# Layer 0's exponentials: from four shared PSUM banks to five SBUF tiles of their own

## The chip, the core and the metric

The kernel runs on one core of one Trainium2 chip. The metric is the device time of one execution in microseconds, from launch to the end of the last instruction; lower is better. Times before are of three runs and of one more execution that the hardware profiler recorded. Engines: PE is TensorE (PEld its weight loads), DVE is VectorE, ACT is ScalarE, POOL is GpSimd, SP is SyncE, which here only issues DMAs.

## The reference

Four layers run one after the other over an image tensor `x` of 4 x 64 x 64 x 128 in float32, each as `x = x + layer(groupnorm(x))`. Only layer 0 is touched. It is a selective scan over the image in four directions:

```python
def step(h, xs):
    ut, dt, bt, ct = xs
    dA = jnp.exp(dt[..., None] * A)
    h = dA * h + (dt * ut)[..., None] * bt[:, :, None, :]
    y = jnp.einsum('bkdn,bkn->bkd', h, ct)
    return (h, y)
```

There are 256 channels `d`, 16 states `n` for each, four directions `k` (rows, columns, and both backwards) and 4096 positions, for each of four images. In front of the scan stand a projection, a 3x3 convolution for each channel and a SiLU; `delta` is a softplus. Behind it the four directions are summed, normalized over the channels, gated and projected. Layers 1 to 3 (Fourier layers and attention) follow.

## The kernel before

**Tiling.** Layer 0 (`layer0`) works in units: image `b`, direction `k` (in the order 1, 3, 0, 2), chunk `c` of `CH` = 512 positions: 4 x 4 x 8 = 128 units. Channels lie on the 128 partitions in two halves `s`. Inside a unit a loop runs over the 16 states `n`; each pass of it is called a step here, 2048 in all. A step does:

- POOL: `dB = du * Bb` for both halves at once (line 413), 128x1024. `du` is `delta * u`, made once for each unit (line 299). `Bb` is a row of B broadcast to all partitions by a DMA, four states at a time (three buffers); `dB` has three buffers.
- ACT: for each half `dA = exp(delta * A)` (line 420), 128x512.
- DVE: for each half one scan instruction (line 421), `h[t] = dA[t] * h[t-1] + dB[t]`, from `dA` and `dB`, starting from `state`, a column in SBUF. `h` lies in SBUF, three buffers of four states.
- PE and ACT, seven steps later (`LAG`): `transpose` turns `h` (line 318, PE, into PSUM; line 322, ACT, copies `hT` to SBUF), and `products` multiplies with `W`, which holds C (line 363), into `yT`.

At four steps of a unit PE makes `cr` (line 433), and DVE makes `W` from it (line 436). The next unit's inputs are prepared in between: `xd_ps` (line 277, PE), its copy `xd` (line 279, ACT), `dp` (line 286, PE), `delta` (lines 292 and 293 on ACT, 296 on DVE), `du` (POOL). After each group of four states POOL copies the last column of `h` into `state` (lines 446 and 451). `before(b + 1)` (normalization, projection, convolution of the next image) and `after(b)` (line 236, a normalization on DVE; line 250, `yg`, a product on POOL; the output projection) are generators, of which the loop takes a piece at most steps.

**Buffers.** PSUM has eight banks. Pool `ps` holds two for the transposes, `psy` two for `yT`. Pool `psx` holds four under the one tag `x`: `dA` takes two tiles a step out of it, and `cr`, `xd_ps`, `dp` and the small matmuls of `before` and `after` take theirs from the same four in turn. A new tile of a tag waits until the readers of the tile four places before it are done. SBUF tiles come from `tmp`.

```python
        tmp = pool("l0tmp", 2)
        ...
        ps = pool("l0ps", 2, space=PSUM)
        psx = pool("l0psx", 4, space=PSUM)
        psy = pool("l0psy", 1, space=PSUM)
```

**Order.** The loop is inside `tc.manual_schedule(engines=order)` for PE, ACT, DVE and POOL: each of these runs its instructions in the order of the code, and an instruction that waits holds up everything behind it on its engine. DMAs are issued by SP's queue, whose order a scheduler sets.

Of the kernel before, what the change touches and what calls it, by code (L numbers as in the profile page):

```python
# [10 lines left out]
F32 = mybir.dt.float32  # L11
# [5 lines left out]
P = 128  # L17
# [5 lines left out]
CH = 512  # L23
# [58 lines left out]
def layer0(sh, A, x_in, x_out, scr):  # L82
# [6 lines left out]
    with ExitStack() as ctx:  # L89
        pool = lambda name, bufs, **kw: ctx.enter_context(tc.tile_pool(name=name, bufs=bufs, **kw))  # L90
        wp = pool("l0w", 1)
        tmp = pool("l0tmp", 2)
        small = pool("l0small", 2)
        ps = pool("l0ps", 2, space=PSUM)
        psx = pool("l0psx", 4, space=PSUM)
# [168 lines left out]
        def fetch(b, k, c):  # L264

            u = tmp.tile([P, 2, CH], F32, name="u")
            pc = NCH - 1 - c if k >= 2 else c
            nc.sync.dma_start(
                u, scr(f"xw{b % 2}" if k % 2 else f"xr{b % 2}")[:, :, pc * CH : (pc + 1) * CH].rearrange("s p t -> p s t")
            )  # L270
            return u, (u[:, :, ::-1] if k >= 2 else u)

        def inputs(k, c, u):

            xd_ps = psx.tile([40, CH], F32, name="xd_ps", tag="x")
            for s in range(2):
                nc.tensor.matmul(xd_ps, lhsT=w_x[:, s, k, :], rhs=u[:, s, :], start=(s == 0), stop=(s == 1))  # L277
            xd = xds[c % 2]
            nc.scalar.copy(xd[0:40, :], xd_ps)  # L279
            bd = scr(f"B{(NCH * k + c) % 3}")  # L280
            nc.sync.dma_start(bd, xd[8:24, :])
            yield
            dps = []
            for s in range(2):
                dp = psx.tile([P, CH], F32, name="dp", tag="x")
                nc.tensor.matmul(dp, lhsT=w_dt[:, k, s * P : (s + 1) * P], rhs=xd, start=True, stop=True)  # L286
                dps.append(dp)
                yield
            delta = tmp.tile([P, 2, CH], F32, name="delta")

            for s in range(2):
                nc.scalar.activation(delta[:, s, :], dps[s], AF.Exp)
            nc.scalar.activation(delta, delta, AF.Ln, bias=1.0)
            yield
            for s in range(2):
                nc.vector.scalar_tensor_tensor(delta[:, s, :], delta[:, s, :], 88.0, dps[s], ALU.min, ALU.max)  # L296
            yield
            du = tmp.tile([P, 2, CH], F32, name="du")
            nc.gpsimd.tensor_tensor(du, delta, u, ALU.mult)  # L299
            yield xd, bd, delta, du  # L300
# [24 lines left out]
        def transposed(G):  # L325

            nonlocal copied
            todo, copied = copied, None
            if G is not None:
                q = G["q"]  # L330
                G["q"] += 1
                hTs = [transpose(G, q, 0)]
                copied = G, q, hTs
            yield
            if todo is not None:
                products(*todo)
            if G is not None:
                hTs.append(transpose(G, q, 1))
            yield
# [49 lines left out]
        with tc.manual_schedule(engines=order):  # L389
            for i, (b, k, c) in enumerate(units):  # L390
# [14 lines left out]
                for n in range(NS):  # L405
                    g, q = divmod(n, 4)
                    if q == 0:
                        Bb = tmp.tile([P, 4, CH], F32, name="Bb", bufs=3)
                        nc.sync.dma_start(Bb, bd[4 * g : 4 * g + 4, :].partition_broadcast(P))
                        h = tmp.tile([P, 2, CH, 4], F32, name="h", bufs=3)  # L410
                        G = dict(unit=unit, g=g, h=h, q=0)
                    dB = tmp.tile([P, 2, CH], F32, name="dB", bufs=3)
                    nc.gpsimd.tensor_tensor(dB, du, Bb[:, q : q + 1, :].to_broadcast([P, 2, CH]), ALU.mult)  # L413
                    behind = iter(())
                    if NS * i + n >= LAG:
                        H = queue[0]
                        behind = transposed(H)
                    for s in range(2):
                        dA = psx.tile([P, CH], F32, name="dA", tag="x")
                        nc.scalar.activation(dA, delta[:, s, :], AF.Exp, scale=A_neg[:, k, s, n : n + 1])  # L420
                        nc.vector.tensor_tensor_scan(  # L421
                            h[:, s, :, q], dA, dB[:, s, :], state[:, s, n : n + 1], ALU.mult, ALU.add
                        )
                        next(behind, None)
                    if n == 1:
                        for f in ends.pop("state", []):
                            f()
                    if queue and queue[0]["q"] == 4:
                        queue.pop(0)
                    if n in (1, 5, 11, 13):  # L430
                        crg = (1, 5, 11, 13).index(n)
                        cr = psx.tile([P, CH], F32, name="cr", tag="x")
                        nc.tensor.matmul(cr, lhsT=sel[:, crg, :], rhs=xd[0:40, :], start=True, stop=True)  # L433
                    if n in (2, 6, 12, 14):
                        W = tmp.tile([P, 16, 32], F32, name="W", bufs=3)
                        nc.vector.tensor_tensor(  # L436
                            W,
                            cr.rearrange("p (a t) -> p a t", t=32),
                            diag[:, int(rev) : int(rev) + 1, :].to_broadcast([P, 16, 32]),
                            ALU.mult,  # L440
                        )
                        Ws[crg] = W
                    if q == 3:
                        queue.append(G)
                    if c < NCH - 1 and q == 2 and g > 0:
                        nc.gpsimd.tensor_copy(state[:, :, 4 * g - 4 : 4 * g], last[:, :, CH - 1, :])
                    if q == 3:
                        last = h
                        if g == 3 and c < NCH - 1:
                            ends["state"] = [  # L450
                                lambda st=state, l=h: nc.gpsimd.tensor_copy(st[:, :, 12:16], l[:, :, CH - 1, :])
                            ]

                    if i + 1 < len(units):
                        if n == 3:
                            u_next, v_next = fetch(*units[i + 1])
                        if n in (7, 8, 9):
                            coming = coming or inputs(*units[i + 1][1:], v_next)
                            next(coming)
                        if n in (10, 11):  # L460
                            next(coming)
                        if n == 15:
                            ready = next(coming)

                    if n == 10:
                        y = unit["y"] = tmp.tile([P, 4, 2 * P], F32, name="y", tag="t4", bufs=4)
                        if k == 0:
                            src = scr("y3").rearrange("(w q r) d -> r w q d", w=64, r=2)
                            for r in range(2):
                                nc.sync.dma_start(y[64 * r : 64 * r + 64], src[r, :, 4 * c : 4 * c + 4, :])  # L470
                        elif k != 1:
                            nc.sync.dma_start(y, dst(1 if k == 3 else 0))

                    if n not in (1, 5, 8, 9, 11, 13) and pieces:
                        if next(pieces[0], None) is None:
                            pieces.pop(0)
# [1239 lines left out]
```

## Time and profile before

| | us |
|---|---|
| median of three runs | 9474.88 (9465.93 to 9475.91) |
| profiled execution, its own time | 9466.91 |
| its span, first to last instruction | 9465.1 |
| stretch of layer 0's scans, 218.6 to 6968.7 | 6750 |
| mean granted TensorE clock | 0.889 |

Busy time of the engines, over the span and in the stretch of the scans:

| engine | span, us | stretch of the scans, us |
|---|---|---|
| PE | 7878.8 (83%) | 5817.4 |
| DVE | 7035.5 (74%) | 5736.7 |
| ACT | 6403.3 (68%) | 5370.6 |
| POOL | 5610.1 (59%) | 5237.7 |

A line of the costliest groups gives source line, engine, operation, output and inputs with their tile names, shapes, how often it ran, then after the bar busy time in us and the mean duration of one in ns, then the idle time of the engine just in front of these instructions and what ended most of it. A line of a timeline gives start and duration in us, engine, line and operation; in brackets stands idle time in front. In a tile's answer, three durations are minimum, median and maximum in ns. An instruction's duration in this profile includes time in which it has been started and is held up inside its engine, so a longer duration is not always more work. Layer 2's helper records each of its operations under line 785, so its groups are told apart by tile names.

### The profile page before, as it was taken

The numbers are of one execution on the slowest core, as the hardware profiler recorded it, in microseconds if no ns is written. First come the engines' busy times: TensorE is split into PE (matmuls) and PEld (weight loads), VectorE is DVE, ScalarE is ACT, GpSimd is POOL, SyncE is SP. The second block draws the span as 40 slices with busy tenths as digits, with TensorE's granted clock in tenths as the row PEclk, the third lists the DMA queues.
The fourth block names the chain that finished last, engine by engine and source line by source line (L and its number), as shares of the span: only waits on it lengthen the run. The fifth ranks groups of instructions, "written<-read, shape, count | busy, mean of one in ns | idle before, by whom it ended". The sixth has DMA issues, their size and how long they took to land. (4 is left out here: it accounts for less than half of the span.)

```text
span 9465.1 us, 144952 instructions
## 1 busy us (share of the span) xinstructions
PE 7878.8 (83%) x54256; PEld 4499.6 (48%) x54256; DVE 7035.5 (74%) x8298; ACT 6403.3 (68%) x11773; POOL 5610.1 (59%) x2998
## 2 busy tenths in 40 slices
PE   7888888888888888888888888888869967677588
PEld 3444444444444444444444444444447756365366
DVE  1778788898887788888777898998954553443578
ACT  2878787777787777778777777888842211614467
POOL 1777778877777777777777878888840001010133
PEclk8989998888898998889999898999979988778699
DMA  6334443333444443334434333333332124131333
GB/s 112 110 115 127 115 128 123 113 121 128 125 126 118 117 122 115 136 121 119 118 118 126 110 137 123 130 128 114 131 116 53 35 59 132 51 103 50 88 87 86
DMA packets 1148677, 1038.13 MB, mean 110 GB/s; under 512 B 564127, under 2 KB 1001979, under 8 KB 1081156
## 3 DMA queue, kind: packets, MB, share of 16 engines
q1 hardware_dynamic: 1146292, 1027.13, 35.7%
q8 instruction: 426, 6.98, 0.3%
q14 instruction: 279, 2.29, 0.1%
q10 hardware_dynamic: 1680, 1.74, 0.1%
HBM read 845.18 MB, written 181.32 MB: 108 GB/s over the span
## 5 line engine op out<-in xcount | busy, mean ns | idle before, releaser
L421 DVE TENSOR_TENSOR_SCAN h<-dA,state,dB 128x512 f32<-128x512 f32 x4096 | 4998.3, 1271 | 1003.1 <-ACT dA L420 786.5
L413 POOL TENSOR_TENSOR dB<-du,Bb 128x1024 f32<-128x1024 f32 x2048 | 4829.1, 2374 | 1413.6 <-DVE h L421 1146.7
L420 ACT ACTIVATE dA<-delta,A_neg 128x512 f32<-128x512 f32 x4096 | 2864.3, 699 | 505.2 <-DVE h L421 428.5
L318 PEld LDWEIGHTS pt<-ident,h 128*128 128x128 f32 x16384 | 1948.6, 150 | 2008.3 <-issue 1303.5
L318 PE MATMUL pt<-ident,h 128*128 128x128 f32 x16384 | 2756.7, 299 | 103.8 <-ACT hT L322 103.8
L322 ACT COPY hT<-pt 128x512 f32<-128x512 f32 x4096 | 2416.9, 590 | 588.5 <-PE pt L318 552.9
L363 PE MATMUL yT<-hT,W 128*32 128x256 f32 x16384 | 1660.3, 418 | 18.0 <-ACT hT L322 15.2
L433 PE MATMUL cr<-xd,sel 40*128 40x512 f32 x1024 | 667.6, 736 | 460.5 <-DVE h L421 456.3
L363 PEld LDWEIGHTS yT<-hT,W 128*32 128x32 f32 x16384 | 409.7, 111 | 576.2 <-issue 374.0
L193 PE MATMUL cv<-pad,taps 128*128 128x512 f32 x1152 | 608.2, 629 | 0.0
L433 PEld LDWEIGHTS cr<-xd,sel 40*128 40x128 f32 x1024 | 169.4, 207 | 565.8 <-DVE h L421 514.4
L785 POOL TENSOR_TENSOR xg<-xg,so 128x1024 f32<-128x1024 f32 x8 | 26.6, 3343 | 693.4 <-ACT so L785 672.3
L1434 POOL TENSOR_TENSOR S<-S,sm 128x784 f32<-128x784 f32 x128 | 191.1, 1493 | 408.7 <-DVE sm L1432 348.4
L277 PE MATMUL xd_ps<-u,w_x 128*40 128x512 f32 x512 | 281.5, 678 | 134.2 <-DVE h L421 106.1
L286 PE MATMUL dp<-xd,w_dt 65*128 65x512 f32 x512 | 282.2, 634 | 113.6 <-DVE h L421 112.8
L299 POOL TENSOR_TENSOR du<-delta,u 128x1024 f32<-128x1024 f32 x128 | 304.0, 2375 | 66.3 <-DVE delta L296 66.3
L436 DVE TENSOR_TENSOR W<-cr,diag 128x512 f32<-128x512 f32 x512 | 341.4, 667 | 0.0
L785 POOL TENSOR_TENSOR z<-z,sp 128x1024 f32<-128x1024 f32 x16 | 41.8, 2616 | 465.4 <-ACT z L785 465.1
L1441 ACT ACTIVATE S<-S,mx 128x196 f32<-128x196 f32 x512 | 227.9, 448 | 33.9 <-DVE mx L1468 33.4
L785 PE MATMUL pz<-PT,WX 128*68 128x64 f32 x2048 | 167.1, 248 | 100.0 <-DVE WX L785 81.4
L193 PEld LDWEIGHTS cv<-pad,taps 128*128 128x128 f32 x1152 | 197.1, 203 | 106.1 <-issue 99.4
L279 ACT COPY xd<-xd_ps 40x512 f32<-40x512 f32 x128 | 74.3, 580 | 223.2 <-PE xd_ps L277 223.2
(333 smaller groups left out, 7785.7 us busy)
## 6 DMA issues: line engine op xcount, KB each, us to landing
Bb<-l_B SPq DMA_DIRECT2D x512, 1024.0 KB
l_y<-y SPq DMA_DIRECT2D x128, 512.0 KB
wr<-wt SPq DMA_DIRECT2D x256, 136.0 KB
u<-l_xw SPq DMA_DIRECT2D x64, 512.0 KB
y<-l_y SPq DMA_DIRECT2D x64, 512.0 KB
u<-l_xr SPq DMA_DIRECT2D x64, 512.0 KB
V<-l_v SPq DMA_DIRECT2D x512, 49.0 KB
l_xr<-xo SPq DMA_DIRECT2D x64, 256.0 KB
```

The lines of the kernel that those rows point to most:

```text
L193: nc.tensor.matmul(pm, lhsT=taps[:, s, t, :], rhs=pad[:, s, dy : dy + 8, dx : dx + 64], start=(t == 0), stop=(t == 8),)
L277: nc.tensor.matmul(xd_ps, lhsT=w_x[:, s, k, :], rhs=u[:, s, :], start=(s == 0), stop=(s == 1))
L286: nc.tensor.matmul(dp, lhsT=w_dt[:, k, s * P : (s + 1) * P], rhs=xd, start=True, stop=True)
L299: nc.gpsimd.tensor_tensor(du, delta, u, ALU.mult)
L318: nc.tensor.transpose(pt[:, r, s, :], G["h"][:, s, t0 : t0 + 32, :].rearrange("p t n -> p (t n)"), sh.ident)
L322: nc.scalar.copy(hT, pt.rearrange("p r s d -> p r (s d)"))
L363: nc.tensor.matmul(U["yT"][e][32 * jo : 32 * jo + 32, qo % 2, :], lhsT=U["Ws"][G["g"]][:, 4 * q + j, :], rhs=hTs[j // 2][:, j % 2, :], sta ...
L413: nc.gpsimd.tensor_tensor(dB, du, Bb[:, q : q + 1, :].to_broadcast([P, 2, CH]), ALU.mult)
L420: nc.scalar.activation(dA, delta[:, s, :], AF.Exp, scale=A_neg[:, k, s, n : n + 1])
L421: nc.vector.tensor_tensor_scan(h[:, s, :, q], dA, dB[:, s, :], state[:, s, n : n + 1], ALU.mult, ALU.add)
L433: nc.tensor.matmul(cr, lhsT=sel[:, crg, :], rhs=xd[0:40, :], start=True, stop=True)
L436: nc.vector.tensor_tensor(W, cr.rearrange("p (a t) -> p a t", t=32), diag[:, int(rev) : int(rev) + 1, :].to_broadcast([P, 16, 32]), ALU.mult,)
```

## The change

One line: `dA` is no longer a tile of the PSUM pool `psx` under the tag `x`, but a tile of the SBUF pool `tmp` with a tag of its own and five buffers. The exponential writes there, and the scan reads it from there. `psx` keeps its four banks, which now serve `cr`, `xd_ps`, `dp` and the other small matmuls alone. The order of instructions on PE, ACT, DVE and POOL is the same in both kernels; on SP some DMAs change places.

```diff
                     for s in range(2):
-                        dA = psx.tile([P, CH], F32, name="dA", tag="x")
+                        dA = tmp.tile([P, CH], F32, name="dA", bufs=5)
                         nc.scalar.activation(dA, delta[:, s, :], AF.Exp, scale=A_neg[:, k, s, n : n + 1])
                         nc.vector.tensor_tensor_scan(
                             h[:, s, :, q], dA, dB[:, s, :], state[:, s, n : n + 1], ALU.mult, ALU.add
                         )
```

## The prediction

> **What bounds the kernel now.** I read the costliest groups first, then the answers for the tiles `dA` and `dB`, then the timeline of VectorE and GpSimd. Layer 0's scans run from 218.6 to 6968.7 us: 6750 us of the 9465.1 us span, 2048 steps of 3.30 us. A step is one POOL product `dB` (line 413), two exponentials on ScalarE (line 420), two scans on VectorE (line 421), and TensorE's transposes and products. Groups: busy us and mean ns, then the idle time in front.
>
> ```profile
> L421 DVE TENSOR_TENSOR_SCAN h<-dA,state,dB 128x512 f32<-128x512 f32 x4096 | 4998.3, 1271 | 1003.1 <-ACT dA L420 786.5
> L413 POOL TENSOR_TENSOR dB<-du,Bb 128x1024 f32<-128x1024 f32 x2048 | 4829.1, 2374 | 1413.6 <-DVE h L421 1146.7
> L420 ACT ACTIVATE dA<-delta,A_neg 128x512 f32<-128x512 f32 x4096 | 2864.3, 699 | 505.2 <-DVE h L421 428.5
> ...
> L433 PE MATMUL cr<-xd,sel 40*128 40x512 f32 x1024 | 667.6, 736 | 460.5 <-DVE h L421 456.3
> ```
>
> No engine is full in the 6750 us: PE is busy 5817, VectorE 5737, ScalarE 5371, POOL 5238. They wait on each other in a ring. VectorE waits for `dA` (786 us); ScalarE waits for a PSUM bank that a scan still reads (428 us); PE's small matmuls `cr`, `xd_ps` and `dp` wait for the same four banks (456 + 106 + 113 = 675 us), and while PE's queue stands, the transposes behind it stand too. The change addresses these 428 and 675 us.
>
> What also matters is something the ring doesn't show: 2 x 1.271 us of scan and 2.374 us of `dB` sum to 4.92 us, yet a step takes 3.30. So scans and `dB` overlap freely now. The tile answer for `dB` says so again (duration min/median/max): neither is ever held up by the other.
>
> ```profile
> L421 DVE TENSOR_TENSOR_SCAN h<-dA,state,dB x4096: 1247/1267/1325, 218.6 to 6967.4; 128x512 f32<-128x512 f32 x196
> L413 POOL TENSOR_TENSOR dB<-du,Bb x2048: 2333/2373/2547, 216.2 to 6960.6; 128x1024 f32<-128x1024 f32 x187
> ```
>
> Today a scan reads `dA` from PSUM and only `dB` from SBUF. In layer 2 VectorE multiplies two SBUF tensors while POOL does the same. The two timelines there (start, duration):
>
> ```profile
> 8225.61 1.23 DVE L785 TENSOR_TENSOR m<-m,z 128x1024 f32<-128x1024 f32 x1 [1.44 <-POOL z L785]
> ...
> 8228.30 1.82 DVE L785 TENSOR_TENSOR m<-m,q 128x1024 f32<-128x1024 f32 x1
> ```
> ```profile
> 8223.23 2.35 POOL L785 TENSOR_TENSOR z<-z,sp 128x1024 f32<-128x1024 f32 x1 [200.97 <-ACT z L785]
> 8226.31 2.73 POOL L785 TENSOR_TENSOR z<-z,sp 128x1024 f32<-128x1024 f32 x1 [0.73 <-ACT z L785]
> ```
>
> POOL's second `z` starts at 8226.31, inside VectorE's `m` (to 8226.84), and takes 2.73 us where the first, alone, took 2.35: it ends 2.20 us after VectorE does. VectorE's next `m` starts at 8228.30, inside that `z` (to 8229.04), and takes 1.82 where the one before took 1.23: it ends 1.08 us after POOL. Each stood still until the other was through, and each saved about 0.14 us of its own length, its start having been done while it waited. The groups `xg` and `Z` show the same, a VectorE `xg` lasting 1202/1225/3357 ns (min/median/max). And line 236, a one-source VectorE operation from SBUF to SBUF, lasts 381/409/2599 ns in layer 0, beside `dB`.
>
> **What the skill says.** The Trainium skill, "SBUF — State Buffer", section "Who interferes with whom": an instruction of VectorE with two SBUF inputs contends with a GpSimd instruction that reads SBUF, because its second input comes through the read interface that they share; the second to come fully blocks until the first ends. The trace agrees in layer 2 (2.73 and 1.82 us above) and, for one SBUF input, in layer 0 (1.27 beside 2.37 us, no block). The same section counts line 236's kind, in a two-port mode, among the blockers, as its 2599 ns shows. "ScalarE: Activation LUTs", section "Step-by-step: what each stage is for", calls PSUM the nearer destination for ScalarE; the trace can price that (below), at nothing.
>
> **The change part by part.**
>
> *Bank waits go.* `dA` leaves the tag `x`; the small matmuls have the four banks to themselves. In the order of instructions, `cr`, `xd_ps` and `dp` lose their wait on VectorE. Gain at most 675 us, if PE sets the pace.
>
> *`dA` on ScalarE.* Rows from SBUF to SBUF: 128x128 in 388 ns (`m<-z,A`), 128x196 in 446 ns (`S<-S,mx`), so 0.85 ns an element and 446 + 316 x 0.85 = 715 ns for 512, against 699. 4096 x 16 ns = 66 us, on an engine that is 80% busy in the stretch: hidden, more so in a longer step. With that cover gone it costs 66 us.
>
> *The scan's own length.* 128x512 from PSUM and SBUF takes 667 ns (`W`, line 436), from two SBUF tensors 692 (`ot<-ot,x`, line 1412). I take 25 ns more: 1.296 us; bounds 0 and 50.
>
> *The new wait.* The scan now has two SBUF inputs, and every `dB` reads SBUF. If they exclude each other as `m` and `z` do, a step is a sum. `dB` has three buffers, so POOL waits for the release of one, takes the interface at the next scan's end, and the next scan waits for it: scan, scan, `dB`. `dB` costs 2.374 - 0.14 = 2.23; the scan behind it 1.296 - 0.14 = 1.16; the scan behind a scan its pitch of today, 1.19 (eight back to back took 9.50 us), + 0.025 = 1.21. Together 4.60 us; x 2048 = 9421 us.
>
> To it, on the same interface: `du` (line 299) 128 x 2.23 = 286; `yg` (line 250) 32 x 2.22 = 71; 448 copies of the state, 0.19 - 0.14 = 0.05 each, 22; line 236's 128 at 0.409 - 0.14, 34. Sum 9834 us. VectorE's other work in the stretch, 5737 - 4998 - 136 (line 236) = 603 us of `W`, `delta`, `y` and statistics, has at most one SBUF tensor source; it runs while POOL holds the interface, which it does for some 2.2 us in every step. A tenth of it left over: 60. Stretch 9.89 ms, against 6.75: **+3.14 ms**.
>
> *What stands behind it.* On VectorE every scan blocked holds up `W`, `delta` and `y` behind it; on POOL, the copies of the state. ScalarE's `dA` and PE's transposes wait for scans, but need only 5371 and 5817 us of 9890. POOL's `Bb` (145 us of DMA waits now) has three buffers of four steps, 18 us of use each instead of 13. SP's queue issues the same transfers; some loads and stores of `y` and `Bb` change places, at DMA 38% busy and falling: nothing. The bank waits are then covered entirely.
>
> Sum against the profiled execution: 9466.9 (span 9465.1) + 3140 = **12,607 us, say 12,600**. The median of the runs is 8 us above that execution, far inside the error.
>
> **Rivals.**
>
> *The scan is not held up: faster.* No row shows a scan with both tensors in SBUF beside POOL; it moves an element in 2.4 ns where a product takes 1.2, and might fetch otherwise. Then only the waits go: at best all 675 us of PE's, leaving PE 5817 + 258 of other waits, so 8,790 us; since ScalarE waits 525 us for transposes and VectorE needs 5737 anyway, half is likelier: 9,130. It decides if scan and `dB` keep 1.27 and 2.37 us with overlap. Against it: every VectorE product of two SBUF tensors beside POOL in layer 2 was held.
>
> *The interface is shared read by read.* POOL's 2048 reads in 2.37 us are 1.16 ns each; a scan adds 512, 0.59 us; a step is 2.37 + 1.19 = 3.56, 7290 us, with `du`, `yg` and copies 7.7 ms: 10,400. Against it: `m` ended 1.08 us after `z`, the remainder of a whole instruction.
>
> *Longer exclusion.* No start is saved: 2.374 + 2 x 1.296 = 4.97, x 2048 = 10,170, others 304 + 75 + 87 + 52: 10,690, so 13,400; with none of the 603 us hidden 14,010. Against it: the 0.14 us seen at each hand-over.
>
> *The edit does nothing*, because the waits only change their name and the scan isn't held: 9,467.
>
> **How the numbers follow.** Exclusion, in its two forms, 0.87: likeliest 12,600, from 12,450 (no 25 ns, nothing left over) upward. Sharing read by read 0.05; faster 0.06; no change 0.02. The range reaches from 12,300, which allows 0.18 instead of 0.14 us saved at each of the two hand-overs of a step and no 25 ns, to 13,400, no start saved. The chances are against 0.2%, 19 us, about what a measurement can tell: faster 0.06, same 0.01, slower 0.93.
>
> **What would show it.** A held instruction's wait counts as its duration: scans should last about 1.2 and 3.4 us in turn (mean 2.2 to 2.5), `dB` 3.3 to 3.6; VectorE's digits in layer 0 go to 9, PE's fall to 5 or 6; `cr`'s wait for scans vanishes; `W` stays at 0.67; layers 1 to 3 are as before. Scans at 1.3 with `dB` at 2.4 and a step under 3.3 us would prove me wrong.

## The result, and the profile after

The changed kernel takes 12,482.67 us (median of four runs, 12,470.16 to 12,487.24) against 9472.73 (four runs): a ratio of 1.3177, 95% interval 1.3154 to 1.3199. The predicted time was 12,600. The layers behind layer 0 are unchanged; its scans now run from 218.3 to 9989.2 us, 9771 us where it was 6750.

The costliest groups of the changed kernel (busy us, mean ns, then idle time in front and what ended it):

```profile
L421 DVE TENSOR_TENSOR_SCAN h<-dA,state,dB 128x512 f32<-128x512 f32 x4096 | 8914.6, 2237 | 135.5 <-POOL dB L413 94.9
L413 POOL TENSOR_TENSOR dB<-du,Bb 128x1024 f32<-128x1024 f32 x2048 | 5788.5, 2829 | 2757.7 <-DVE h L421 1968.1
L420 ACT ACTIVATE dA<-delta,A_neg 128x512 f32<-128x512 f32 x4096 | 2961.7, 723 | 3229.0 <-DVE h L421 3218.7
...
L433 PE MATMUL cr<-xd,sel 40*128 40x512 f32 x1024 | 738.8, 809 | 282.6 <-DVE delta L296 240.8
...
L446 POOL COPY state<-h 128x8 f32<-128x8 f32 x336 | 368.9, 1098 | 0.0
...
L436 DVE TENSOR_TENSOR W<-cr,diag 128x512 f32<-128x512 f32 x512 | 337.2, 659 | 0.0
```

The same scan of 512 elements is "busy" 2237 ns instead of 1271, `dB` 2829 instead of 2374, and a copy of eight columns 1098 instead of 194. `W`, with `cr` in PSUM and only one input in SBUF, stays at 0.66. ScalarE now waits 3219 us for scans to give its tiles back (429 before): it is behind VectorE, which is busy or held up for 9633 of the 9771 us. What the change was for did happen: `cr` no longer waits for scans (456 us before; what is left is a wait for `delta`).

The tile answer for `dB` (durations in ns: minimum/median/maximum):

```profile
L421 DVE TENSOR_TENSOR_SCAN h<-dA,state,dB x4096: 1179/2474/3431, 218.3 to 9988.0; 128x512 f32<-128x512 f32 x196
L413 POOL TENSOR_TENSOR dB<-du,Bb x2048: 2337/3175/3401, 215.9 to 9979.3; 128x1024 f32<-128x1024 f32 x187
```

The timeline of two steps, VectorE and then POOL (start, duration in us):

```profile
4000.78 1.25 DVE L421 TENSOR_TENSOR_SCAN h<-dA,state,dB 128x512 f32<-128x512 f32 x1
4001.96 3.32 DVE L421 TENSOR_TENSOR_SCAN h<-dA,state,dB 128x512 f32<-128x512 f32 x1
4005.20 1.25 DVE L421 TENSOR_TENSOR_SCAN h<-dA,state,dB 128x512 f32<-128x512 f32 x1
4006.37 3.30 DVE L421 TENSOR_TENSOR_SCAN h<-dA,state,dB 128x512 f32<-128x512 f32 x1
...
4001.00 3.20 POOL L413 TENSOR_TENSOR dB<-du,Bb 128x1024 f32<-128x1024 f32 x1 [1.22 <-issue]
4005.42 3.17 POOL L413 TENSOR_TENSOR dB<-du,Bb 128x1024 f32<-128x1024 f32 x1 [1.23 <-DVE h L421]
```

Read it as turns. The scan of 4000.78 runs free and ends at 4002.03. `dB`, started at 4001.00, gets its turn then and ends at 4004.20, 2.17 us later. The next scan, started at 4001.96, moves only now and ends at 4005.28, 1.08 us after `dB`. A step from scan to scan is 4005.20 - 4000.78 = 4.42 us, and nothing of the three overlaps but their starts. Not every step looks like this. Over the whole trace 2139 of the 4096 scans last over 1.5 us, none before, and 1133 of the 2048 `dB` over 2.6 us, of which all but three start while a scan is still running. The other `dB` start beside `W`, `y`, `delta` or other small work, or beside nothing, and last 2.35 us.

### The profile page after: what moved, and what is told of

Its sections match the earlier page's. It is cut to its first block, busy times and chain, and to the rows that moved or that the text cites. A ratio compares the mean times of both kernels' runs of the same rounds, so it can differ in the third digit from the quotient of the medians.

```text
span 12482.9 us, 145476 instructions
## 1 busy us (share of the span) xinstructions
PE 9245.9 (74%) x54256; PEld 5043.1 (40%) x54256; DVE 10930.3 (88%) x8298; ACT 6526.1 (52%) x11773; POOL 7093.4 (57%) x2998
## 5 line engine op out<-in xcount | busy, mean ns | idle before, releaser
L421 DVE TENSOR_TENSOR_SCAN h<-dA,state,dB 128x512 f32<-128x512 f32 x4096 | 8914.6, 2237 | 135.5 <-POOL dB L413 94.9
L413 POOL TENSOR_TENSOR dB<-du,Bb 128x1024 f32<-128x1024 f32 x2048 | 5788.5, 2829 | 2757.7 <-DVE h L421 1968.1
L420 ACT ACTIVATE dA<-delta,A_neg 128x512 f32<-128x512 f32 x4096 | 2961.7, 723 | 3229.0 <-DVE h L421 3218.7
L318 PE MATMUL pt<-ident,h 128*128 128x128 f32 x16384 | 3262.8, 338 | 642.8 <-ACT hT L322 638.7
L318 PEld LDWEIGHTS pt<-ident,h 128*128 128x128 f32 x16384 | 2295.1, 171 | 2963.9 <-issue 1653.5
L363 PE MATMUL yT<-hT,W 128*32 128x256 f32 x16384 | 2311.4, 484 | 1104.9 <-ACT hT L322 830.8
L322 ACT COPY hT<-pt 128x512 f32<-128x512 f32 x4096 | 2340.5, 572 | 644.6 <-PE pt L318 635.6
L363 PEld LDWEIGHTS yT<-hT,W 128*32 128x32 f32 x16384 | 510.8, 121 | 2048.7 <-ACT hT L322 1306.0
L299 POOL TENSOR_TENSOR du<-delta,u 128x1024 f32<-128x1024 f32 x128 | 415.5, 3246 | 66.3 <-DVE delta L296 66.3
L446 POOL COPY state<-h 128x8 f32<-128x8 f32 x336 | 368.9, 1098 | 0.0
L451 POOL COPY state<-h 128x8 f32<-128x8 f32 x112 | 104.2, 931 | 261.9 <-DVE h L421 261.9
```

What stands on the lines that cost most here:

```text
L318: nc.tensor.transpose(pt[:, r, s, :], G["h"][:, s, t0 : t0 + 32, :].rearrange("p t n -> p (t n)"), sh.ident)
L322: nc.scalar.copy(hT, pt.rearrange("p r s d -> p r (s d)"))
L363: nc.tensor.matmul(U["yT"][e][32 * jo : 32 * jo + 32, qo % 2, :], lhsT=U["Ws"][G["g"]][:, 4 * q + j, :], rhs=hTs[j // 2][:, j % 2, :], sta ...
L421: nc.vector.tensor_tensor_scan(h[:, s, :, q], dA, dB[:, s, :], state[:, s, n : n + 1], ALU.mult, ALU.add)
```

## The experiments

**Taking the read of SBUF away from POOL.** e7 and e8 are e2 and e3 again, timed. The edit in both pairs, on the kernel before (e2, e7) and on the changed one (e3, e8):

```diff
-                    nc.gpsimd.tensor_tensor(dB, du, Bb[:, q : q + 1, :].to_broadcast([P, 2, CH]), ALU.mult)
+                    for _ in range(3):
+                        nc.gpsimd.memset(dB, 0.0)
```

> The kernel before with POOL's product dB replaced by three fills of the same tile with zero (each estimated at 0.78 us from the fills of 20 and 132 columns, 136 and 208 ns, so 2.3 us together, as long as the product); dB is not computed, and POOL reads no SBUF for it. It is the partner of the next run. Both theories: about as before, 9,300 to 9,500 us, scans 1.27 us.

> The changed kernel (dA in SBUF) with the same three fills in place of the product dB. Theory (only POOL instructions that read SBUF exclude a scan with two SBUF inputs): the loss is gone; scans fall from a mean of 2.24 to 1.30 us, and the time is at or below that of the partner with dA in PSUM, by up to 675 us, since the bank waits are gone too. Rival (any POOL instruction excludes the scan, or the scan is slow of itself): 12,000 us or more, scans above 2 us.

> e2 again, timed: dA in PSUM, dB not computed but filled three times with zero. As e2: 9,498 us within 30.

> e3 again, timed: dA in SBUF, dB not computed but filled three times with zero. As e3: 9,288 us within 30, so 1.8 to 2.6% under its partner with dA in PSUM. That difference is what leaving the banks to the small matmuls is worth when no scan is held.

Measured: 9497.9 and 9288.3 us (one run each), and again 9506.07 (ratio to before 1.0031, 1.0022 to 1.0040) and 9266.36 (0.9777, 0.9760 to 0.9793). The tile answer for `dB` in e8, with `dA` in SBUF:

```profile
L414 POOL MEMSET dB<- x6144: 941/952/1097, 1.1 to 6776.7; 128x1024 f32 x199
L422 DVE TENSOR_TENSOR_SCAN h<-dA,state,dB x4096: 1245/1267/3412, 214.3 to 6778.9; 128x512 f32<-128x512 f32 x196
```

POOL is busy with `dB` for as long as in the changed kernel (3 x 0.95 us a step), writes the same tile, and the scan reads the same two SBUF tiles; yet the median scan is back at 1267 ns and the loss of 3010 us is gone. So neither the scan's own length nor POOL's writes hold a scan up: it is POOL's reading of SBUF beside a scan with two SBUF inputs. One trace shows both: in e8 4069 of the 4096 scans run beside a fill, yet only 149 last over 1.5 us, the longest 3412 ns, and beside every one of these runs a POOL product that reads SBUF: `du` beside 125, `yg` beside the other 24. A POOL instruction of another kind that reads SBUF is held too: of the 448 copies of the state 42 last over 0.8 us in e8, each beside a scan, and none over 0.36 in e7, where `dA` is in PSUM. The pair also gives a price for what the change was after: with no scan held by `dB`, emptying the banks is worth 9506 - 9266 = 240 us, 2.5%. That is the price beside fills, and perhaps a low one: in e8 POOL is busy for 6271 of the stretch's 6566 us, and VectorE waits 359 us for its fills, where the kernel before waited 140 for the product.

**Half of the scans.** e1 puts `dA` in SBUF for one half only:

```diff
-                        dA = psx.tile([P, CH], F32, name="dA", tag="x")
+                        if s == 0:
+                            dA = tmp.tile([P, CH], F32, name="dA", bufs=5)
+                        else:
+                            dA = psx.tile([P, CH], F32, name="dA", tag="x")
```

> Only the half s = 0 writes dA to SBUF (five tiles), s = 1 keeps its PSUM tile: half as many scans with two SBUF inputs. Theory (a scan with two SBUF inputs and a dB exclude each other, whole instruction by whole instruction): only one scan of a step is held, the other runs beside dB. A step is 2.23 (dB) + 1.16 (the held scan) = 3.39 us, 6.94 ms for 2048, with du, yg and the copies 0.41 more: 7.36 ms against 6.75 before, so about 10,080 us (10,000 to 10,400); the longest scans of s = 0 reach 3.4 us, none of s = 1 passes 1.35. Rival (read by read sharing, or scans that are slower of themselves when they read two SBUF tensors): half of the loss of the full change stays, about 10,970 us, and scans of s = 0 are lengthened evenly, by some 1 us each.

Measured: 10,634 us (ratio 1.1216, 1.1193 to 1.1238), between the two. Its timeline, VectorE and then POOL, at a step without and one with `W` in between:

```profile
4023.50 1.25 DVE L424 TENSOR_TENSOR_SCAN h<-dA,state,dB 128x512 f32<-128x512 f32 x1
4024.67 0.66 DVE L439 TENSOR_TENSOR W<-cr,diag 128x512 f32<-128x512 f32 x1
4025.26 3.08 DVE L424 TENSOR_TENSOR_SCAN h<-dA,state,dB 128x512 f32<-128x512 f32 x1
...
4003.83 3.27 POOL L413 TENSOR_TENSOR dB<-du,Bb 128x1024 f32<-128x1024 f32 x1
4007.07 3.27 POOL L413 TENSOR_TENSOR dB<-du,Bb 128x1024 f32<-128x1024 f32 x1
...
4024.89 2.35 POOL L413 TENSOR_TENSOR dB<-du,Bb 128x1024 f32<-128x1024 f32 x1 [2.40 <-DVE h L424]
4029.65 2.36 POOL L413 TENSOR_TENSOR dB<-du,Bb 128x1024 f32<-128x1024 f32 x1 [2.40 <-DVE h L424]
```

Where the scan of `s = 0` is already running when `dB` starts, `dB` waits for its end (and so lasts 3.27 us) and then runs beside the free scan, and the next scan of `s = 0` ends 1.08 us behind `dB`: 4007.07 - 4003.83 = 3.24 us a step. Where `W` stands at that place, `dB` finds the interface free and starts at 4024.89, the scan behind `W` stands until `dB` is through (3.08 us), and POOL then idles 2.40 us, since all its buffers are full until the free scan has ended: 4029.65 - 4024.89 = 4.76 us. My 3.39 us knew only the first kind. If so, the halves' places matter:

> As e1, but the halves change places: s = 1 writes dA to SBUF, s = 0 keeps PSUM. e1 came out at 10,634 us, 550 above its expectation, and its timeline shows two kinds of step: 3.24 us where the held scan of s = 0 follows the scan of s = 1 at once, and 4.76 us where W, y or delta stands between them, because then dB, released by the scan of s = 1, takes the interface first and s = 0 waits for all of it. Theory (who comes first at the release decides): now the scan behind the release is the free one, dB always starts 0.2 us behind the release and s = 1 always ends 1.08 us behind dB, whether or not W stands between; a step is 3.6 us throughout, with du, yg and copies 7.74 ms, in all about 10,460 us (10,350 to 10,550), and no step of 4.7 us is left beside W. Rival (only the number of scans with two SBUF inputs counts): 10,634 us within 40.

Measured: 10,318 us (1.0884, 1.0863 to 1.0906), 317 below e1 with the same number of scans in SBUF. The rival, that only the number counts, falls. The level is 30 us under my range, and the shape I gave is not right either. The 1124 steps in which VectorE does nothing else last 3.23 us at the mean (3.36 in e1), and the 923 with other work 4.29 (4.48 in e1). So about half of the gain lies in steps without `W` or `delta`, where my theory saw none. That the place counts is shown; why is only in part, for PE also waits less for scans in front of `cr`, 229 us for 401 in e1.

**Seven of 32.**

```diff
-                        dA = psx.tile([P, CH], F32, name="dA", tag="x")
+                        if s == 1 and n in (1, 5, 7, 8, 9, 11, 13):
+                            dA = tmp.tile([P, CH], F32, name="dA", bufs=5)
+                        else:
+                            dA = psx.tile([P, CH], F32, name="dA", tag="x")
```

> Of a unit's 32 dA tiles only the seven of s = 1 at n = 1, 5, 7, 8, 9, 11, 13, where a small matmul takes a bank in the same step, lie in SBUF: the bank in question is then one that was left half a step earlier. Theory: the bank waits of PE largely go, and seven scans of a unit can be held by dB, each by up to 1.1 us on the mean: 896 such scans, 0 to 990 us lost against 60 to 200 gained (what e4 and the fills showed for the waits): 9,450 to 10,100 us, likeliest 9,700. Rival (few held scans are hidden in VectorE's idle time of some 1000 us, so that the gain is left): 9,280 to 9,420 us, a version better than both.

Measured: 9652.93 us (1.0187, 1.0170 to 1.0204), inside the theory's wide range. Of the 896 scans with two SBUF inputs 682 last over 1.5 us, together 624 us beyond a free scan's 1267 ns, and the kernel is 178 us slower: so the held time is in part hidden or paid for by emptier banks, but not all of it.

**The bank waits by order alone.** `dA` stays in PSUM; `cr` is issued behind the first half of the next step, `xd_ps` and `dp` likewise:

```diff
                         next(behind, None)
+                        if s == 0 and cr_due is not None:
+                            nc.tensor.matmul(cr, lhsT=sel[:, cr_due, :], rhs=xd[0:40, :], start=True, stop=True)
+                            cr_due = None
+                        if s == 0 and n in (8, 9, 10) and coming is not None:
+                            next(coming)
...
                         cr = psx.tile([P, CH], F32, name="cr", tag="x")
-                        nc.tensor.matmul(cr, lhsT=sel[:, crg, :], rhs=xd[0:40, :], start=True, stop=True)
+                        cr_due = crg
```

(`inputs` has a `yield` more behind each of its PSUM tiles.)

> The kernel before (dA in PSUM) with its small matmuls cr, xd_ps and dp issued half a step later in PE's order, behind the transposes of the next step's first half; their banks are taken in the same order as before, so what waits on the banks is the same, only PE comes to them later. Tells what the bank waits were worth by themselves. Theory (the waits hold PE, and PE holds the ring): half to all of the 675 us, so 8,800 to 9,150 us. Rival (PE would only wait elsewhere, for h or for hT): 9,400 to 9,480 us, with PE's idle time in front of pt and yT larger by what is gone in front of cr.

Measured: 9418.60 us (0.9929, 0.9913 to 0.9946), faster than both kernels but far from 8,800 to 9,150. Waits in the stretch of the scans (us in total, times, longest), in the kernel before:

```profile
ACT hT L322 <- PE pt L318: 547.7, 806, 2.5
...
PE cr L433 <- DVE h L421: 456.3, 145, 10.6
...
PE pt L318 <- ACT hT L322: 103.8, 57, 3.0
```

and in e4:

```profile
ACT hT L324 <- PE pt L320: 790.5, 909, 4.7
...
PE pt L320 <- ACT hT L324: 345.1, 196, 4.6
...
PE cr L428 <- DVE h L423: 161.5, 161, 11.8
...
PE cr L428 <- DVE delta L298: 128.4, 45, 3.2
```

In front of `cr` PE waits 290 us instead of 456, but 345 instead of 104 in front of `pt`, and ScalarE waits 791 instead of 548 for `pt`. Most of what went in front of `cr` came back elsewhere in the ring, and the time lies in the rival's range; 0.7% is left.

**Fewer tiles.** The changed kernel with `bufs=2` for `bufs=5`.

> The changed kernel with two SBUF tiles for dA instead of five. Theory (the interface is what scans and dB take in turn; ScalarE has 3,200 us of slack in front of dA): unchanged, 12,480 us within 1%. Rival (the loss comes from the ring of buffers: ScalarE, PE and the scans wait on each other in a new way that the number of dA tiles sets): fewer tiles cost more, 12,700 us or above.

Measured: 12,509.92 us (ratio to before 1.3208, 1.3169 to 1.3246). The number of tiles is not what costs: the intervals of five and of two tiles overlap.

**A term of the sum.** The changed kernel, with `if n == 2:` in front of the making of `W`.

> The changed kernel with W made once in a unit, at n = 2, and used for all four groups of states, where the reference needs four different ones: three of four W, 384 in all, are left out of VectorE's queue (253 us of work at 0.66 us); all else is issued as before. Settles a term of the sum: I took VectorE's other work, 603 us with at most one SBUF tensor, to be nine tenths hidden beside dB. Hidden as put down: 25 us gained, about 12,455 us. Not hidden (the trace has steps without such work at 4.51 us and steps with it at 5.09 on the mean): each W left out gives 0.35 to 0.58 us, 130 to 225 us in all, 12,260 to 12,350 us.

Measured: 12,385.89 us (ratio to before 1.3052, 1.3030 to 1.3074), 97 us under the changed kernel: 97 / 384 = 0.25 us for each `W` of 0.66. The two were run at different times, and by their ratios to the kernel before, run beside each, it is 0.31. So 38 to 47% of a `W` is on the path: neither a tenth nor nearly all.

## Why the prediction was right

**The new wait.** Right in its mechanism: scan, scan, `dB` in turn, each start saved at a hand-over. The fills show the cause. They also exclude the new ring of buffers, which e8 has with no loss, and e9 excludes the number of tiles. The price rises with the number of scans in SBUF, from 7 of 32 (e6, 1.019) over half (e5 and e1, 1.088 and 1.122) to all (1.318). The Trainium skill's page "SBUF — State Buffer", section "Who interferes with whom", names both sides of it: a GpSimd instruction that reads SBUF contends, one that only writes does not. The fills (scans 1267 ns at the median) and the product (2474) agree with it.

**Sizes.** The stretch came out at 9771 us against 9894 in my sum, so close by luck: errors of some hundreds of us nearly cancel. The step was put at 4.60 us and is 4.42 where nothing else comes in (the median of the 1124 steps without other VectorE work is 4.41, their mean 4.51): `dA` in SBUF does not lengthen a free scan by 25 ns, it lasts 1.25 us where the median before was 1.27; and 2.17 and 1.08 us stand for `dB` and the scan behind it, for 2.23 and 1.16. That is 0.18 x 2048 = 369 us too much. VectorE's other work I took to be nine tenths hidden; if e10's 38% held for all of it, 229 of 603 us would not be, in place of 60: 169 too little. 9894 - 369 + 169 = 9694, 77 us short. But this does not close the sum. The share was measured for `W` alone, and it differs by the work: steps with the two `delta` instructions last 5.53 us at the mean, 1.02 more than steps with none, for 1.34 us of work. The turns of `du` and of the copies of the state, which I put at 2.23 and 0.05 us each, were not measured alone either.

**Signs in the profile.** Scans at a mean of 2.24 us, free ones at 1.25 and held ones at 3.3, as put down. `dB` was to last 3.3 to 3.6 and has a mean of 2.83: its median, 3.18, is the held one, but where it starts beside `W`, `y` or `delta` it runs at once and lasts 2.35. PE's digits were to fall to 5 or 6 and stand at 7 (see below). `dA` on ScalarE was worked out at 715 ns and has a median of 722. The bank waits of `cr` on scans went, as expected (456 us before, about 2 now).

**The rivals.** "Not held up" and "read by read" fall on the timeline: each instruction waits for the whole of the other. "Longer exclusion" falls too: `dB` ends 2.17 us behind the scan where it lasts 2.35 alone, and the scan 1.08 behind `dB` for 1.25, so a start of 0.17 to 0.18 us is saved at each hand-over. The gain in the first rival, 340 to 675 us, is not confirmed: beside the fills the empty banks are worth 240 us, but there POOL is nearly full, and no run here shows what they would be worth beside a product that holds no scan. One argument against it was put too strongly: in layer 2 not every VectorE product beside POOL was held. Where VectorE came first, as at 8225.61, it was POOL's product that waited.

## What to carry to other kernels

Before moving an operand of a VectorE instruction from PSUM to SBUF, count its SBUF inputs: if the move makes two, and GpSimd reads SBUF tensors at the same time, the two engines take turns as they did here, and their times add where they overlapped. A PSUM bank held for such an operand may be the cheaper price. And a wait of many microseconds on one engine in a ring of four is no promise of a gain: e4 took 166 us from in front of `cr` and got 63 us for the kernel (9481 for the kernel before, run beside it).

## What the runs showed of the hardware that was not expected

TensorE's granted clock was lower where it had less to do. In the stretch of the scans it was 0.91 before, 0.78 in the changed kernel, with 84 GB/s of DMA for 121, and 0.94 in e8, the fastest. Over the whole run it was 0.889, 0.791 and 0.910. PE shows 7176 us of busy time in the changed kernel's stretch for the same instructions that took 5817 before, and its mean `pt` matmul rose from 299 to 338 ns. Why the clock fell, and how much of the longer busy time is due to it, is not shown by any run here. The fills hold no scan, but they do hold one other VectorE instruction: `yf` (line 236), from SBUF to SBUF, has a median of 409 ns in the kernel before and of 961 and 962 in e7 and e8. POOL's fill of 1024 columns took 0.95 us, for 0.78 worked out from narrow ones.
